# A gather kernel with a sort in front: sort operands made one step ahead, a new dealing of projection blocks, transfers in program order, finer pieces in a compaction, and the last blocks stored singly

## The chip, the core and the metric

The kernel runs on one core of one Trainium2 chip. The metric is the device time of one execution in microseconds (us): the median of three runs before the change is 1930.67 us (1929.54 to 1931.28). The core has five engines that run in parallel, each with its own queue of instructions in a fixed order: PE (TensorE, matrix products), DVE (VectorE), ACT (ScalarE), POOL (GpSimd) and SP (SyncE, which here only starts transfers). An instruction waits at the head of its queue until the semaphores that it needs are set, and everything behind it on that engine waits too.

## The reference, cut to what matters

There are 8192 nodes with 512 features, and 131072 edges sorted by `dst`. The part that the change touches is the graph layer:

```python
def _L0_gnn_ref(x, weight, row, col, vals):
    h = jnp.einsum('nf,ef->ne', x, weight)
    msgs = vals[:, None] * h[col]
    out = jax.ops.segment_sum(msgs, row, num_segments=N_NODES)
    return out
...
x = x + _L0_gnn_ref(_layernorm(x, axis=-1), L0_gnn_weight, src, dst, edge_weight)
x = x + _L0_ffn_ref(_layernorm(x, axis=-1)[None], L0_ffn_W, L0_ffn_b)[0]
```

Every node is normalised and projected to h. Then each edge gathers row `dst` of h, scales it by the edge's weight and adds it to node `src`. Edges come sorted by `dst`, and the sum runs over `src`: the kernel must first sort the edges by `src`. The second layer, a small network on each node's features, follows.

## The kernel before

Nodes lie in 64 blocks of 128. The edges of a block are handled as tiles of 128 slots: 17 tiles for each block, 1088 in all, dealt in two parts (`TILES`: 6 tiles of each block in part 0, 11 in part 1). A tile is one gather of 128 rows of h by POOL (`rows_for`, L519), one selection matrix `hot` made by DVE (`hots_for`, L530), and one 128x512 product on PE (L804). The edges are sorted in two parts as well: part 0 of the sort must be complete before the first gather, part 1 before the first tile of part 1.

The program has three stages in time.

*Head.* `project` computes h for 64 blocks. For a pair of blocks, `load` (L451, SP) fetches 512 KB of x, `scale` takes the statistics on DVE (L459, L460, L171, L463) and normalises on ACT (L170, L465). For each block, `turn` transposes on PE (L474) and copies back on ACT (L476); then come the product on PE (L492), a copy out of PSUM on ACT (L494), and for every second block a store of the pair to `h_rows` (L496, SP). `scale` of a pair is called two blocks ahead of its use, `turn` one block ahead. Steps of the generator `order(0)`, the sort's part 0, are put between these blocks.

*First half of the tiles.* `begin` runs part 0's 384 tiles and puts steps of `order(1)` between them, one step at a tile number `due` that each step moves on (by 3 for `STEP`, 4 for `SLOW`).

*Second half.* `evenly` runs part 1's 704 tiles and the second layer between them.

`order(part)` is a number of chunks, 7 in part 0 and 9 in part 1, followed by `squeeze`. A chunk (`chunk`) makes a one-hot `hot` (L251, DVE), sums it over partitions (L259, PE, copied on ACT at L261), runs a cumulative sum on DVE (L264, L266), takes ranks (L271 on PE, L275 and L277 on DVE), then makes `at` for the whole chunk at once (L281, DVE). Four times over (`SUB` of 2 out of `GC` = 8) it makes `blocks` (L288, ACT), two halves of `put` (L295, DVE), and after the next step 64 short products p_c (L308, PE). `blocks` and `put` have two buffers each. `squeeze` compacts what the chunks placed: a scan (L323), and for each of ten bits a shift (L375), a mask operation (L381), a copy on ACT (L379) and two predicated copies (L387), all but the copy on DVE. `parts` says into how many pieces DVE's instructions are cut: 1 for all of part 0; for part 1, 8 in the chunks and 4 in `squeeze`. At its end `squeeze` transposes the results (L421).

PE, DVE and ACT run in the order in which the program is written. SP and POOL are not in that list (`manual_schedule`, L535): a scheduler decides their order. In the head, a credit says how many steps of the sort go behind each block: 6 for a block from the third on, a step of a chunk costs 3 (two steps for each block), a step of `squeeze` costs 6 (one for each block). The gathers' tiles, x's pairs and h's blocks share one pool of six buffers (`gp`); `gw`, the projection's weights, has one of the two buffers of `xp1`, in which `begin` keeps its x.

Of the kernel before, what the change touches and what calls it, by code (L numbers as in the profile page):

```python
# [17 lines left out]
PE, DVE, ACT = mybir.EngineType.PE, mybir.EngineType.DVE, mybir.EngineType.Activation  # L18

# [14 lines left out]
def tile_gnn_ffn(  # L34
# [51 lines left out]
    STEP, SLOW = 3, 4  # L86
# [158 lines left out]
    def chunk(ck, ps_c, q, col, parts):  # L245
# [9 lines left out]
        yield STEP  # L255
# [6 lines left out]
        yield STEP  # L262
# [4 lines left out]
        yield STEP  # L267
# [5 lines left out]
        yield STEP  # L273
# [5 lines left out]
        for cs in cut(CG, parts):  # L279
            n = cs.stop - cs.start  # L280
            nc.vector.tensor_tensor(  # L281
                at[:, cs].rearrange("p n h s -> p n (h s)"),
                lots.rearrange("p (o h) s -> p o (h s)", o=1).to_broadcast([P, n, CAP]),
                slot[:, cs].to_broadcast([P, n, CAP]), OP.is_equal)
        p_c = None
        for c0 in range(0, GC, SUB):
            blocks = ck.tile([P, SUB, GQ, NB], F32, name="blocks", bufs=2)
            nc.scalar.copy(blocks, hot[:, c0 : c0 + SUB].rearrange("p c b g -> p c g b"))  # L288
            put = ck.tile([P, SUB * GQ, 2, 2, HALF], F32, name="put", bufs=2)
            for i, val in enumerate((val_a, val_w)):  # L290
                for cs in cut(SUB, min(parts, SUB)):
                    n = (cs.stop - cs.start) * GQ
                    v = val[:, q, c0 + cs.start : c0 + cs.stop, :].rearrange(
                        "p c (g a b) -> p (c g) a b", a=1, b=1)
                    nc.vector.tensor_tensor(  # L295
                        put[:, cs.start * GQ : cs.stop * GQ, :, i, :],
                        at[:, (c0 + cs.start) * GQ : (c0 + cs.stop) * GQ],
                        v.to_broadcast([P, n, 2, HALF]), OP.mult)
            yield STEP
            if p_c is None:  # L300
                p_c = ps_c.tile([P, GQ, 2, HALF], F32, name="p_c")
                nc.tensor.matmul(p_c.rearrange("p g w s -> p (g w s)"), nil[:, :P], nil,
                                 start=True, stop=False)
            for k in range(SUB * GQ):
                c, g = divmod(k, GQ)
                last = c0 + SUB == GC and k == SUB * GQ - 1
                for h in range(2):
                    nc.tensor.matmul(p_c[h * NB : (h + 1) * NB, g], blocks[:, c, g, :], put[:, k, h],  # L308
                                     start=False, stop=last)
        for i, cells in enumerate((cells_a, cells_w)):  # L310
# [3 lines left out]
    def squeeze(part, sq, ps_q, parts):  # L314
# [19 lines left out]
        yield SLOW  # L334
# [8 lines left out]
        yield SLOW  # L343
# [22 lines left out]
        yield SLOW  # L366
        wt = cells_w
        for bit in range(LOW, LOW + BITS):
# [14 lines left out]
            yield SLOW  # L383
# [5 lines left out]
            yield SLOW  # L389
# [25 lines left out]
        yield SLOW  # L415
        for f, to in ((dst_f, at_dst[part]), (row_f, at_row[part]), (w_c, at_w[part])):
# [12 lines left out]
            yield SLOW  # L429

    def order(part):
# [7 lines left out]
        with tc.tile_pool(name="sq", bufs=1) as sq, \  # L439
                tc.tile_pool(name="ps_q", bufs=2, space=PSUM) as ps_q:  # L440
            yield from squeeze(part, sq, ps_q, (fine + 1) // 2)


    def project():
# [37 lines left out]
        for b in range(NB):  # L482
# [12 lines left out]
            if b % 2:  # L495
                nc.sync.dma_start(rows_of(h_rows, b - 1, 2), t[:, 2:4])  # L496
                del pairs[b - 1], parts[b - 1]
# [37 lines left out]
    man_ctx.enter_context(tc.manual_schedule(engines={PE, DVE, ACT}))  # L535
    first, second, heads = order(0), order(1), project()
    LEAD, MORE = 2, 2 * STEP
    credit, early = 0, 0
    for b, _ in enumerate(heads):
        credit += MORE if b >= LEAD else 0  # L540
        while credit > 0 and first:
            n = next(first, None)
            if n is None:
                first = None
            else:
                credit -= n if n == STEP else MORE
        if first is None and early < AHEAD:
            hots_for(early)
            early += 1
    assert first is None  # L550
# [257 lines left out]
    def begin():  # L808
# [3 lines left out]
        def load(b0):  # L812
            t = xp1.tile([P, G, D], F32, name="xg")
            nc.sync.dma_start(t, rows_of(x, b0, G))
            return t

# [7 lines left out]
        xs, last = {0: load(0)}, None  # L824
        for b, k, p_g in blocks_of(0):
            t = b * TILES[0] + k
            if k == AFTER and b % G == 0 and b + G < NB:
                xs[b // G + 1] = load(b + G)
            if k == AFTER and last:
                add(*last)  # L830
            if k == TILES[0] - 1:
                last = (b, p_g)
            if t == due:
                due += next(second, NB * FT)
# [249 lines left out]
```

## Time and profile before

| | |
|---|---|
| median of three runs | 1930.67 us |
| the profiled execution | 1927.51 us, 1.8 us of it around its span |
| its span | 1925.7 us |
| busy shares | PE 88%, POOL 58%, DVE 52%, ACT 20% |
| L519 gathers, POOL | 1088 of 1013 ns, 743.4 us idle before them, 691.6 us of it "issue" |
| L804 tile products, PE | 2176 records (two for each tile), 1071.9 us busy |
| L492 projection, PE | 512 records (eight for each block), 238.3 us busy |
| L308 p_c, PE | 4096 records, 140.4 us busy, 28.9 us idle before them |
| L288 blocks, ACT | 64 of 2075 ns |
| store of a pair of h, 512 KB | 3.0 us to landing (median) |
| load of x in `begin`, 1024 KB | 9.1 us to landing (median) |

A line of a timeline reads: start, duration, engine, line, operation, what it writes and reads, shapes, how many were merged, and in brackets the idle time before it and what ended it. A line of the waits reads: who waited for whom, total us, times, longest. A line of the windows reads: the stretch, its length, then for each engine busy us and instructions, TensorE's granted clock, the DMA engines' share and GB/s. The first L251 of the sort starts at 28.99 us, the last product of the head ends at 418.7 us, the first gather starts at 427.14 us, the last gather at 1871.7 us. The span before the first gather is the head; in 427 to 780 us the chunks of part 1 run, from 780 to 905 us its `squeeze`.

### The profile page before, as it was taken

Reading aid. Unit: us, or ns where it says so; the run is one execution under the profiler, and the core shown is the slowest. Engines: PE = TensorE matmul, PEld = TensorE weight load, DVE = VectorE, ACT = ScalarE, POOL = GpSimd, SP = SyncE. Lnnn points to the kernel's source line nnn. Section 1 sums busy time; section 2 is a strip of 40 time slices with the busy share of each in tenths; the row PEclk is TensorE's granted clock in tenths of the full one; section 3 lists DMA queues with packets and bytes.
Section 4 is the critical chain, followed back from the end, with each engine's and each line's share of the span. In section 5 each row is a group of like instructions: output and inputs, shape, how many; then the busy total and the mean of one; then the engine's idle time right before and its main releaser. Section 6 shows DMA issues by size and latency. Waiting matters only on the chain.

```text
span 1925.7 us, 24263 instructions
## 1 busy us (share of the span) xinstructions
PE 1695.5 (88%) x9288; PEld 819.9 (43%) x9288; DVE 1008.2 (52%) x2710; ACT 389.3 (20%) x520; POOL 1124.8 (58%) x1138
## 2 busy tenths in 40 slices
PE   5888889969999999878878789898988989899996
PEld 2554554434455455323333334343434434343454
DVE  5556558635886886985323344435344443434432
ACT  3444545532222222111000011020100101010211
POOL 4000000017777777887777777777777777777760
PEclk9899999989999999978999999899999999999996
DMA  5112223337777777668889777878787787878770
GB/s 177 61 51 67 67 66 115 126 116 219 255 245 237 254 223 223 212 195 257 273 253 321 211 209 223 286 210 295 209 287 220 238 263 209 275 210 274 239 236 25
DMA packets 140908, 391.38 MB, mean 203 GB/s; under 512 B 20336, under 2 KB 21360, under 8 KB 140784
## 3 DMA queue, kind: packets, MB, share of 16 engines
q0 software_dynamic: 87952, 286.45, 49.3%
q1 hardware_dynamic: 52304, 102.25, 15.2%
q8 instruction: 76, 1.25, 0.3%
q10 hardware_dynamic: 528, 1.05, 0.2%
q14 instruction: 48, 0.39, 0.1%
HBM read 339.33 MB, written 50.33 MB: 202 GB/s over the span
## 4 chain that ended last, share of the span: by engine, by line
PE 40%; POOL 19%; DMA 17%; issue 12%; DVE 9%; ACT 3%; POOLq 0%; DVEq 0%; ACTq 0%; SPq 0%
POOL g L519 19%; DMA g<-h_rows,at_dst 16%; PE p_g L804 16%; PE p_g L492 10%; PE p_c L308 6%; DVE cum L264 2%; DVE cum L266 2%; PE p_g L474 2%; ACT blocks L288 1%; DVE at L281 1%; PE p_base L259 1%; PE p_a L603 1%; PE p_a L601 1%; DVE hot L530 1%; PE p_rank L271 1%
## 5 line engine op out<-in xcount | busy, mean ns | idle before, releaser
L519 POOL DMA_INDIRECT g<-h_rows,at_dst x1088 | 1101.9, 1013 | 743.4 <-issue 691.6
L804 PE MATMUL p_g<-g,hot 128*128 128x512 f32 x2176 | 1071.9, 630 | 1.3 <-DVE xg L819 1.3
L804 PEld LDWEIGHTS p_g<-g,hot 128*128 128x128 f32 x2176 | 400.5, 197 | 385.1 <-issue 371.7
L530 DVE TENSOR_SCALAR hot<-lanes,at_row,at_w 128x128 f32<-128x128 f32 x1088 | 302.8, 361 | 158.7 <-PE p_g L804 152.8
L492 PE MATMUL p_g<-xg,g 128*128 128x512 f32 x512 | 238.3, 610 | 1.1 <-ACT g L476 1.0
L308 PE MATMUL p_c<-put,blocks 128*64 128x40 f32 x4096 | 140.4, 236 | 28.9 <-ACT blocks L288 21.8
L800 PE MATMUL p_j<-g,hot 128*1 128x4 bf16 x272 | 45.7, 168 | 135.9 <-DMA g<-h_rows,at_dst 95.6
L308 PEld LDWEIGHTS p_c<-put,blocks 128*64 128x64 f32 x4096 | 132.9, 145 | 70.6 <-ACT blocks L288 33.8
L288 ACT CAST blocks<-hot 128x1024 f32<-128x1024 bf16 x64 | 130.4, 2075 | 136.9 <-issue 111.8
L800 PEld LDWEIGHTS <-hot 128*1 128x1 bf16 x272 | 21.6, 79 | 317.2 <-issue 284.6
L492 PEld LDWEIGHTS p_g<-xg,g 128*128 128x128 f32 x512 | 95.7, 197 | 100.3 <-issue 96.5
L575 DVE TENSOR_SCALAR hb<-p_b,b_b 128x128 f32<-128x128 f32 (+1 forms) x54 | 18.2, 336 | 218.5 <-PE p_b L595 195.9
L264 DVE TENSOR_TENSOR cum<-cum,hot 128x512 bf16<-128x512 bf16 x112 | 47.7, 426 | 118.5 <-ACT cum L261 115.2
L170 ACT ACTIVATE rstd_f<-mv_f,eps 128x8 f32<-128x8 f32 (+1 forms) x9 | 2.7, 300 | 462.6 <-DVE mv_f L788 462.6
L860 DVE TENSOR_TENSOR xu<-xu,p_g 128x512 f32<-128x512 f32 x64 | 43.7, 683 | 84.5 <-PE p_g L804 84.4
L295 DVE TENSOR_TENSOR put<-at,val_a 128x320 f32<-128x320 bf16 (+1 forms) x100 | 54.9, 578 | 59.1 <-PE p_c L308 58.9
L819 DVE TENSOR_TENSOR xg<-xg,p_g 128x512 f32<-128x512 f32 x64 | 43.8, 684 | 70.9 <-PE p_g L804 70.9
L578 ACT ACTIVATE ha<-p_a,b_a 128x512 f32<-128x512 f32 (+1 forms) x54 | 34.5, 640 | 217.0 <-PE p_a L603 206.3
L474 PE MATMUL p_g<-ident,g 128*128 128x128 f32 x256 | 43.2, 296 | 21.5 <-ACT g L465 21.5
L494 ACT COPY g<-p_g 128x512 f32<-128x512 f32 x64 | 37.5, 586 | 119.1 <-PE p_g L492 119.1
L603 PEld LDWEIGHTS p_a<-hb,w_z 128*128 128x128 f32 x360 | 51.8, 207 | 17.9 <-issue 16.7
L295 DVE TENSOR_TENSOR put<-at,val_w 128x320 f32<-128x320 bf16 (+1 forms) x100 | 55.2, 580 | 0.0
(179 smaller groups left out, 1098.1 us busy)
## 6 DMA issues: line engine op xcount, KB each, us to landing
g<-h_rows,at_dst POOLq DMA_INDIRECT x1088, 4.1
g<-in_x_dram SPq DMA_DIRECT2D x32, 512.0 KB, 4.3
xg<-in_x_dram SPq DMA_DIRECT2D x16, 1024.0 KB, 9.1
h_rows<-g SPq DMA_DIRECT2D x32, 512.0 KB, 3.0
x_rows<-xg SPq DMA_DIRECT2D x32, 512.0 KB, 4.4
xu<-x_rows SPq DMA_DIRECT2D x16, 1024.0 KB, 15.6
out_dram<-xu SPq DMA_DIRECT2D x7, 2048.0 KB, 11.0
xg<-in_gnn_wT_dram ACTq DMA_DIRECT2D x1, 1024.0 KB, 9.0
```

Of the source, the lines that this page charges most:

```text
L264: nc.vector.tensor_tensor(cum[:, c], cum[:, c - 1], hot[:, c - 1], OP.add)
L288: nc.scalar.copy(blocks, hot[:, c0 : c0 + SUB].rearrange("p c b g -> p c g b"))
L295: nc.vector.tensor_tensor(put[:, cs.start * GQ : cs.stop * GQ, :, i, :], at[:, (c0 + cs.start) * GQ : (c0 + cs.stop) * GQ], v.to_broadcast ...
L308: nc.tensor.matmul(p_c[h * NB : (h + 1) * NB, g], blocks[:, c, g, :], put[:, k, h], start=False, stop=last)
L474: nc.tensor.transpose(p_t[:, k * P : (k + 1) * P], t[:, 2 + b % 2, k * P : (k + 1) * P], ident)
L492: nc.tensor.matmul(p_h, t[:, b % 2, k * P : (k + 1) * P], gw[:, k, :], start=(k == 0), stop=(k == KD - 1))
L519: nc.gpsimd.indirect_dma_start(out=g[:, k, :], out_offset=None, in_=h_rows, in_offset=bass.IndirectOffsetOnAxis(ap=at_dst[part][:, i : i + ...
L530: nc.vector.tensor_scalar(hot[:, k, :], lanes, at_row[part][:, i : i + 1], at_w[part][:, i : i + 1], op0=OP.is_equal, op1=OP.mult)
L603: nc.tensor.matmul(p_a[:, g, :], w_z[:, i, g, :], last_hb, start=False, stop=((g + 1) * T % 512 == 0 or g == NG - 1))
L800: nc.tensor.matmul(p_j[:, part, :], hot[:, GS - 1, :].bitcast(BF16)[:, 1:2], g.rearrange("p k d -> p (k d)").bitcast(BF16).rearrange("p (k ...
L804: nc.tensor.matmul(p_g, hot[:, i, :], g[:, i, :], start=(k == 0), stop=(k == TILES[part] - 1))
L819: nc.vector.tensor_add(xg[:, b % G, :], xg[:, b % G, :], p_g)
```

## The change

Five things change, and nothing else.

1. *Operands of p_c.* A new inner function `prepare(c0)` makes the piece of `at` that belongs to `c0`, `blocks` and `put`. Two are prepared before the first p_c, and each p_c run prepares the one two further on. `at` is cut into a quarter of the chunk each time.
2. *Dealing of steps in the head.* Each yield carries a second number, the blocks of h that are to run before the next step. In a chunk: 1 behind `hot`, 0 behind L259, 2 behind the cumulative sum, 0 behind the ranks' products, 2 behind the first two `prepare`, then 0, 1, 0 between p_c runs: six blocks for each chunk. In `squeeze`, half a block for each step. Part 1 still goes by the first number, which is unchanged.
3. *SP in program order.* SP is added to the engines whose order is as written. x's first tile of `begin` is loaded behind block 32 of h; the other loads come behind `add`.
4. *`squeeze` of part 1 in 8 pieces*, not 4. Part 0 stays whole.
5. *Blocks 62 and 63 of h are stored singly*, 256 KB each. (The `del` of two dictionary entries goes too; it issues nothing.)

```diff
-        yield STEP
+        yield STEP, 1
...
         cum = ck.tile([P, GC, NB, GQ], BF16, name="cum")
         nc.scalar.copy(cum[:, 0], p_base)
-        yield STEP
+        yield STEP, 0
...
-        yield STEP
+        yield STEP, 2
         p_rank = ps_c.tile([P, GC, NB // GC, GQ], F32, name="p_rank")
...
-        yield STEP
+        yield STEP, 0
         rank = ck.tile([P, GC, GQ], F32, name="rank")
...
-        for cs in cut(CG, parts):
...
-        p_c = None
-        for c0 in range(0, GC, SUB):
+        ready = {}
+
+        def prepare(c0):
+
+            if c0 >= GC:
+                return
+            n = SUB * GQ
+            n0 = c0 * GQ
+            for cs in cut(n, max(1, parts * SUB // GC)):
+                cs = slice(n0 + cs.start, n0 + cs.stop)
+                m = cs.stop - cs.start
+                nc.vector.tensor_tensor(
+                    at[:, cs].rearrange("p n h s -> p n (h s)"),
+                    lots.rearrange("p (o h) s -> p o (h s)", o=1).to_broadcast([P, m, CAP]),
+                    slot[:, cs].to_broadcast([P, m, CAP]), OP.is_equal)
             blocks = ck.tile([P, SUB, GQ, NB], F32, name="blocks", bufs=2)
             nc.scalar.copy(blocks, hot[:, c0 : c0 + SUB].rearrange("p c b g -> p c g b"))
-            put = ck.tile([P, SUB * GQ, 2, 2, HALF], F32, name="put", bufs=2)
+            put = ck.tile([P, n, 2, 2, HALF], F32, name="put", bufs=2)
...
+            ready[c0] = blocks, put
+
+        prepare(0)
+        prepare(SUB)
+        p_c = ps_c.tile([P, GQ, 2, HALF], F32, name="p_c")
+        yield STEP, 2
+        nc.tensor.matmul(p_c.rearrange("p g w s -> p (g w s)"), nil[:, :P], nil, start=True,
+                         stop=False)
+        for c0 in range(0, GC, SUB):
+            blocks, put = ready.pop(c0)
             for k in range(SUB * GQ):
...
+            prepare(c0 + 2 * SUB)
+            if c0 + SUB < GC:
+                yield STEP, c0 // SUB % 2
...
-        yield SLOW
+        yield SLOW, SHARE
...
-            yield from squeeze(part, sq, ps_q, (fine + 1) // 2)
+            yield from squeeze(part, sq, ps_q, fine)
...
-            if b % 2:
+            if b >= NB - 2:
+                nc.sync.dma_start(rows_of(h_rows, b, 1), t[:, 2 + b % 2 : 3 + b % 2])
+            elif b % 2:
                 nc.sync.dma_start(rows_of(h_rows, b - 1, 2), t[:, 2:4])
-                del pairs[b - 1], parts[b - 1]
...
-    man_ctx.enter_context(tc.manual_schedule(engines={PE, DVE, ACT}))
+    man_ctx.enter_context(tc.manual_schedule(engines={PE, DVE, ACT, SP}))
...
-    LEAD, MORE = 2, 2 * STEP
-    credit, early = 0, 0
+    LEAD = 2
+    due, early = LEAD, 0
     for b, _ in enumerate(heads):
-        credit += MORE if b >= LEAD else 0
-        while credit > 0 and first:
-            n = next(first, None)
-            if n is None:
+        while first and due <= b + 1:
+            step = next(first, None)
+            if step is None:
                 first = None
             else:
-                credit -= n if n == STEP else MORE
+                due += step[1]
...
+        if b == NB // 2:
+            x_0 = load_x(0)
...
-        xs, last = {0: load(0)}, None
+        xs, last = {0: x_0}, None
         for b, k, p_g in blocks_of(0):
             t = b * TILES[0] + k
-            if k == AFTER and b % G == 0 and b + G < NB:
-                xs[b // G + 1] = load(b + G)
             if k == AFTER and last:
                 add(*last)
+            if k == AFTER and b % G == 0 and b + G < NB:
+                xs[b // G + 1] = load_x(b + G)
```

With `SHARE` = 0.5. As built, the changed program's queues differ from the old ones as follows. In the head, PE has a chunk's seven pieces as: L259, two blocks, L271, two blocks, two p_c runs, a block, two p_c runs, and a block before the next L259. On SP, the third pair of x comes before x's first tile of `begin` and no longer behind it, that tile stands between two transfers of the middle of the head, and the last h stores stand in front of the next x load and no longer around it. From there on SP's order is the one of before, and so is POOL's.

## The prediction

> **What bounds the kernel now.** I read the busy time by stage first, to see which engine is full where; then the waits of the stage that the change rewrites; then the timelines at the places where one stage hands over to the next.
>
> ```profile
> core 0: us, PE busy (x) PEld busy (x) DVE busy (x) ACT busy (x) POOL busy (x), PEclk, DMA share, GB/s
> 31.60:276.00 244.40, 206.18 (x2180) 127.43 (x2179) 144.95 (x223) 116.85 (x144) 0.00 (x0) 0.93 0.19 63
> 276.00:418.80 142.80, 138.08 (x474) 67.03 (x472) 95.62 (x197) 72.48 (x129) 0.00 (x0) 0.99 0.34 111
> 427.10:780.00 352.90, 328.08 (x2976) 170.40 (x2977) 259.18 (x704) 84.16 (x64) 268.58 (x247) 0.98 0.76 234
> 780.00:905.00 125.00, 95.87 (x190) 37.87 (x190) 102.82 (x260) 13.13 (x10) 103.07 (x73) 0.85 0.69 215
> 905.00:1872.00 967.00, 875.36 (x3218) 385.60 (x3217) 379.05 (x1254) 82.39 (x136) 729.58 (x770) 0.97 0.80 248
> ```
>
> From 905 us to the last gather POOL issues 770 gathers in 967 us, 1.256 us each, and the waits of that stage say that it waits for nobody; 0.3 us each is its own issue:
>
> ```profile
> POOL g L519 <- issue: 204.1, 670, 0.3
> ```
>
> So the last third of the argument is simple: POOL's chain, once saturated (from about 765 us), carries any earlier or later moment to the end one for one. What counts is when the first gather starts, and what POOL loses before 905 us. Before the first gather PE is the longest engine, but with 38.2 us idle in the stage of the chunks (244.4 - 206.2), at a granted clock of 0.93. Who makes it wait there (the two largest):
>
> ```profile
> PE p_c L308 <- ACT blocks L288: 19.3, 13, 2.5
> PE p_rank L271 <- DVE cum L266: 14.1, 6, 2.4
> ```
>
> **Head, chunks.** Before, one chunk took 34.8 us (L302 starts at 81.73 and again at 116.55 us) with four blocks of h in it. PE's work for a block is 3.44 (L492) + 0.44 (L474) = 3.88 us; L259 and L271 1.74 us each (68.00 to 69.74, 76.12 to 77.86); a p_c run 1.99 us (66.01 to 68.00), four of them; L302 0.25. Chunk with four blocks: 15.5 + 3.5 + 8.0 + 0.25 = 27.2, so 7.6 us lost. After, six blocks: 23.3 + 3.5 + 8.0 + 0.25 = 35.0 us, and the waits go:
> - L271 gets two blocks (7.8 us) instead of one to cover L261, L264 and L266 (0.6 + 3.2 + 2.3 = 6.1 us). Gone.
> - The first p_c runs get two blocks to cover rank, slot, at, put (0.7 + 0.2 + 2 x (0.75 + 1.5) = 5.4 us) and two L288 (4.0 us). Gone. The last two get one block and a p_c run, 5.9 us, against 4.5 us of DVE; ACT's second L288 waits for the second p_c run and ends 2.0 us after it. Gone.
> - New: ACT's two L288 (4.0 us) stand ahead of the copies L476 that PE needs for the next block but one; and the statistics of the next pair stand behind the cumulative sum. Following the queues I get 0.15 + 0.85 + 1.3 = 2.3 us of PE's waiting for each chunk.
> Period 37.4 us (35.0 if nothing waits, 39.5 if these waits double). The first L259 stays where it is, at 31.57 us: before it stand the same three blocks. The last p_c run ends 33.5 us into its chunk: 31.6 + 6 x 37.4 + 33.5 = 289.5 us, against 279.9 before; but 44 blocks of h are behind it instead of 30.
>
> **Head, squeeze.** Here the change turns against itself. Half a block for a step puts one bit of the squeeze on each block:
>
> ```profile
> 299.66 0.74 DVE L375 TENSOR_SCALAR go<-word 128x1120 int32<-128x1120 int32 x1
> 300.44 1.33 DVE L381 SCALAR_TENSOR_TENSOR word<-go,word 128x1120 int32<-128x1120 int32 x1
> 301.68 0.69 DVE L459 BATCH_NORM_STATS2 st_h<-g 128x6 f32<-128x512 f32 x1
> ...
> 304.88 1.44 DVE L387 COPY_PREDICATED word<-go,word 128x1118 int32<-128x1118 int32 x1
> 306.22 1.40 DVE L387 COPY_PREDICATED w<-go,w 128x1118 f32<-128x1118 int32 x1
> 307.65 0.74 DVE L375 TENSOR_SCALAR go<-word 128x1120 int32<-128x1120 int32 x1
> ```
>
> A bit is 2.0 us (299.66 to 301.68) + 2.8 us (304.88 to 307.65) = 4.8 us; the statistics of a pair 2.05 us and 0.36 us for ACT's root. Before, two blocks took 8.0 us and held one bit: 4.8 + 2.05, so DVE fitted. Now two blocks hold two bits: 9.6 + 2.4 = 12.0 us against PE's 7.8. DVE is the bound, since PE's next transposes need the statistics queued behind the bits. On DVE from 290.2 us: three opening steps with one pair's statistics 11.6 us, to 301.8; bits 0 to 9 (seven of 4.8, then 4.5, 4.1, 2.7 by the same rows) with five pairs' statistics, 44.9 + 12 = 56.9 us. The statistics of blocks 56 and 57 are the last that PE waits for, two bits' steps earlier: 356 us; ACT's normalising and transposes, then nine blocks to the end (nine products, eight transposes, 34.5 us), 2 us for L421, and 1 us for the transposes' waits seen before: 394.0 us against 418.7. Gain 24.7 us, of about 38 that the idle time offered.
>
> TensorE's clock drops after gaps: at 380.96 us PE had waited 2.26 us and then 0.52, and the eight products behind it took 5.40 instead of 3.44 us. In the squeeze the gaps are some 4 us for each pair, hidden as DVE is the bound; only the last counts, 2 us at most, within the range.
>
> [...]
>
> **Head, last store and SP.**
>
> ```profile
> 418.76 0.37 SPq L814 DMA_DIRECT2D xg<-in_x_dram  x1
> 419.38 0.36 SPq L496 DMA_DIRECT2D h_rows<-g  x1
> ```
>
> ```profile
> 419.38 6.73 DMA h_rows<-g
> ```
>
> The last store is issued behind a 1 MB load that was waiting for `gw`'s buffer, and lands in 6.73 us where the median is 3.0. After, it stands ahead of that load and is half as long: I take 2.4 us (between 2, and 3.0 for the whole pair alone), a gain of 4.3. The load now meets the first gathers; the first four take 3.85 us to issue and 3.9 to land, so it is nearly past (it took 6.0 us there): 0 to 1 us, I take 0. x's first tile moves from SP's first transfers to block 32: at the start DVE waits only for src (until 5.40 us) and then never for x, so nothing is gained; at block 32 it can make the next pair 3 us late, with 8 us of cover: 0 (at worst 3). SP then waits in order, but for stores and loads in the same order as before: 0.
>
> First gather: 427.1 - 24.7 - 4.3 = 398.1 us. **29.0 us gained.**
>
> **Part 1's chunks.** Steps keep their places. PE loses 7.2 us in nine waits for put (0.8 us each), since all of `at` (3.39 us) stands before the first put; with a quarter of it (0.84) these go. POOL waited 11.8 us for PE's buffers there, some 8 beyond its 0.3 a piece: it can take the gain, from the first such wait at about 650 us. I take 6 us (0 to 8). The wait of L271 stays.
>
> **Part 1's squeeze in eighths.** DVE's predicated copies hold up POOL's gathers:
>
> ```profile
> 827.64 2.01 DVE L387 COPY_PREDICATED word<-go,word 128x388 int32<-128x388 int32 x4
> 827.82 4.51 POOL L519 DMA_INDIRECT g<-h_rows,at_dst  x1 [0.30 <-issue]
> 829.54 2.01 DVE L387 COPY_PREDICATED w<-go,w 128x388 f32<-128x388 int32 x4
> ```
>
> A gather that should take 0.95 us ends 0.9 us after the run's last piece: it got into none of the seven gaps. Seven of ten bits cost 2.8 to 3.7 us so, 23 us in all; two passed (pieces of 384 and 304: 1.15 and 1.23 us at most), and the last lost 1 us (176). Pieces of 196 cost about 0.30 us (four of 176: 1.11 us together, four of 391: 2.03), so a run of 16 takes 4.7 instead of 4.0 us. Bounds: all seven stalls gone, 23 us less; all ten stalled and longer, 10 us more. Nearest row: 176, which still waited to its run's end. I take 1 us more. DVE's own extra, some 1 us a bit, is covered: POOL needs 13.8 us for the eight tiles of a stalled bit (8 x 1.25, 3.3, and 0.5 beside L375), DVE 9.4.
>
> The Trainium skill (SBUF — State Buffer, "SBUF: two separate sides") says that whichever of VectorE's and GpSimd's instructions starts first holds the port pair they share for the whole instruction. Read piece by piece, a gather would wait for one piece only, already at four pieces; the 4.51 us row disagrees. If it held for smaller pieces, the time would be 1873 us.
>
> **Sum.** -24.7 - 4.3 - 6 + 1 = -34.0. The profiled execution, 1927.5, gives 1893.5; the median of the runs lies 3.2 above it: 1930.7 - 34.0 = 1896.7, I say 1896 us. Own range of this case: 1885 to 1908 (half of what the chunk's bounds of 35.0 and 39.5 give over seven, -8 and +7, and 3 to 5 us for part 1).
>
> **Rivals.**
> - *POOL gets in between the smaller pieces* (for: the runs that passed; against: seven that didn't). 24 us less: 1873 us.
> - *DVE-bound squeeze is longer*: pairs of 14.5 us rather than 12, as ACT's copies L379 stand ahead of its root (DVE waited 1.2 us for it, at 296.6 us, before), and the clock lost at 10 us. For: those rows; against: PE's 4 us slack a pair. 6 x 2.5 + 3: about 1914 us.
> - *The dealing doesn't remove the waits*, which move to ACT, the chunk at 42 us: seven times 4.6 more, gain gone: 1928 us.
> - *Slower: eighths starve POOL through the whole bit.* Place: 780 to 905 us. If with twice as many instructions no gather passes during L381's pieces either, each bit blocks 1 + 2.4 + 4.7 = 8 us: 80 us over ten bits instead of 27, so 1896 + 53 = 1949 us. It decides from 3.5 us more a bit. Against: beside L381's four pieces gathers passed at 0.99 and 1.12 us.
>
> **How the numbers follow.** Forecast 0.68, POOL freed 0.12, longer squeeze 0.12, no removal 0.03, starved 0.05. A measurement here can tell 0.2% from no change, 4 us. Faster 0.92, same 0.03, slower 0.05. Range for 8 in 10: from 1876, near the freed case, to 1910, near the longer squeeze.
>
> **What would show it.** The first gather near 398 us (390 to 408); L302 every 37 us with PE's waits for L288 and L266 nearly gone in the chunks; PE waiting for L465 in the squeeze; the last h store landing in under 3 us; no wait for put from there to 780 us minus the shift; POOL still with gathers of over 4 us in L387's runs, or without. The forecast is wrong if the first gather stays above 415 us, or if POOL loses more than 60 us in `squeeze`.

## The result, and the profile after

The changed kernel takes 1902.64 us (median of six runs, 1899.08 to 1906.19), beside 1930.11 us for the kernel before on the same chip: ratio 0.986, 95% interval 0.9843 to 0.9877. The forecast was 1896 us. The profiled executions are 1903.79 and 1927.51 us, their spans 1901.9 and 1925.7 us: 23.8 us less. The medians lie 27.5 us apart: the execution of before that was profiled lies 2.6 us below its median, that of the change 1.2 us above.

To place these 23.8 us I cut both traces at the same gathers of POOL: the first, the 220th after it (the last chunks of part 1's sort), the 320th after it (the end of its squeeze), and the last.

| stretch, us | before | after | difference | forecast |
|---|---|---|---|---|
| start to the first gather | 427.1 | 399.5 | -27.7 | -29.0 |
| 220 gathers on, beside part 1's chunks | 312.6 | 303.4 | -9.2 | -6 |
| the next 100, beside part 1's squeeze | 167.0 | 176.5 | +9.5 | +1 |
| from there to the last gather | 965.0 | 966.4 | +1.4 | 0 |
| last gather to the end | 54.0 | 56.2 | +2.2 | 0 |
| sum | 1925.7 | 1901.9 | -23.8 | -34.0 |

The busy time by stage, after. The first row is the chunks of the head, the second the head's squeeze, then part 1's chunks, its squeeze, and the rest.

```profile
core 0: us, PE busy (x) PEld busy (x) DVE busy (x) ACT busy (x) POOL busy (x), PEclk, DMA share, GB/s
31.60:286.00 254.40, 245.36 (x2405) 142.07 (x2403) 159.42 (x280) 141.07 (x190) 0.00 (x0) 1.00 0.28 93
286.00:395.70 109.70, 88.36 (x251) 41.01 (x249) 85.51 (x161) 47.47 (x82) 0.00 (x0) 0.94 0.24 82
399.40:720.00 320.60, 305.06 (x2805) 159.41 (x2806) 241.15 (x668) 80.99 (x63) 243.80 (x232) 0.98 0.79 246
720.00:880.00 160.00, 119.56 (x372) 49.69 (x371) 129.48 (x428) 18.07 (x18) 126.89 (x89) 0.86 0.66 199
880.00:1846.00 966.00, 869.99 (x3201) 382.13 (x3199) 378.43 (x1251) 81.33 (x132) 728.85 (x768) 0.97 0.79 247
```

In the head's chunks PE's idle time fell from 38.2 to 9.0 us (254.4 - 245.4), and the granted clock rose from 0.93 to 1.00. In the head's squeeze it is the other way: PE had 4.7 us of idle time there before (142.8 - 138.1), now 21.3. The waits of PE up to the last product of h say for whom:

```profile
PE p_g L490 <- ACT g L481: 15.4, 6, 3.4
PE p_g L508 <- ACT g L492: 12.2, 20, 0.8
```

The waits for `blocks` and `cum`, 19.3 and 14.1 us in the chunks before, are gone. The second line is the new wait in the chunks, two short ones (0.52 and 0.78 us) in each chunk, and the 0.52 us behind each longer gap of the squeeze. The first is the squeeze of the head: PE waits for ACT's normalising, which waits for DVE. PE's timeline there (start, duration, engine, line, what; the idle time before it in brackets):

```profile
306.14 0.66 PE L490 MATMUL p_g<-ident,g 128*128 128x128 f32 x4 [2.47 <-ACT g L481]
307.31 5.40 PE L508 MATMUL p_g<-xg,g 128*128 128x512 f32 x8 [0.52 <-ACT g L492]
312.55 0.60 PE L490 MATMUL p_g<-ident,g 128*128 128x128 f32 x4
312.99 3.60 PE L508 MATMUL p_g<-xg,g 128*128 128x512 f32 x8
319.03 0.66 PE L490 MATMUL p_g<-ident,g 128*128 128x128 f32 x4 [2.45 <-ACT g L481]
320.20 3.70 PE L508 MATMUL p_g<-xg,g 128*128 128x512 f32 x8 [0.52 <-ACT g L492]
```

This pair of blocks takes 12.9 us (306.14 to 319.03), and the product behind its gap runs for 5.40 us, the next one for 3.60. Not every gap does that: behind the next, of 2.45 us, the product runs for 3.70 us, and that pair takes 12.1 us (319.03 to 331.13). Of the six gaps for L481 four are followed by a slow product (5.19 to 5.40 us, behind 2.68, 2.47, 3.36 and 2.39 us) and two are not (3.70 us, behind 2.45 and 2.10 us). The five pairs between them take 12.9, 12.9, 12.1, 12.6 and 12.5 us. DVE and ACT in the pair from 306.14:

```profile
305.15 0.74 DVE L391 TENSOR_SCALAR go<-word 128x1120 int32<-128x1120 int32 x1
...
310.24 0.74 DVE L391 TENSOR_SCALAR go<-word 128x1120 int32<-128x1120 int32 x1
...
314.39 1.43 DVE L403 COPY_PREDICATED w<-go,w 128x1116 f32<-128x1116 int32 x1 [0.59 <-ACT w L395]
315.71 0.68 DVE L475 BATCH_NORM_STATS2 st_h<-g 128x6 f32<-128x512 f32 x1
...
318.04 0.74 DVE L391 TENSOR_SCALAR go<-word 128x1120 int32<-128x1120 int32 x1
```

```profile
312.75 0.59 ACT L510 COPY g<-p_g 128x512 f32<-128x512 f32 x1 [3.49 <-PE p_g L508]
313.23 1.13 ACT L395 COPY w<-w 128x1120 f32<-128x1120 f32 x1
317.44 0.29 ACT L171 ACTIVATE rstd_h<-mv_h,eps 128x2 f32<-128x2 f32 x1 [3.08 <-DVE mv_h L476]
```

One bit takes 5.1 us (305.15 to 310.24), the next 5.5 with a wait of 0.59 us for ACT's copy, and the statistics 2.3 us (315.71 to 318.04). DVE is nearly full, as forecast, but each piece is a little longer than I had put it, and ACT's copy for the second bit stands behind the copy of the slow product's result. Of the four pairs with two whole bits (from 306.14, 319.03, 331.13 and 343.76), DVE waits for that copy in the three with a slow product (0.6, 0.4 and 1.3 us) and not in the one from 319.03.

The end of the head, on SP's queue and on POOL:

```profile
396.31 0.33 SPq L512 DMA_DIRECT2D h_rows<-g  x1
396.68 0.43 SPq L557 DMA_DIRECT2D xg<-in_x_dram  x1
399.47 1.01 POOL L536 DMA_INDIRECT g<-h_rows,at_dst  x1 [375.33 <-issue]
```

The last store now goes ahead of the 1 MB load. The first gather starts 3.8 us after h's last product ends (395.65); before it was 8.4 us.

Part 1's squeeze, one bit, DVE and POOL:

```profile
754.53 2.28 DVE L403 COPY_PREDICATED word<-go,word 128x195 int32<-128x195 int32 x8
...
755.52 4.27 POOL L536 DMA_INDIRECT g<-h_rows,at_dst  x1 [0.30 <-issue]
...
756.71 2.28 DVE L403 COPY_PREDICATED w<-go,cells_w 128x195 f32<-128x195 int32 x8
...
758.89 1.11 DVE L547 TENSOR_SCALAR hot<-lanes,at_row,at_w 128x128 f32<-128x128 f32 x4
```

The gather starts among sixteen predicated copies and ends at 759.79, 0.90 us after the operation behind the last of them starts (758.89). Smaller pieces have not let it in. Eight copies take 2.28 us where four took 2.01, and both runs of a bit 4.4 us (754.53 to 758.89) where they took 3.8 (827.64 to 831.43), so the stop is longer. Not every gather in such a run is held: three that start in one (the 277th, 278th and 303rd after the first) take 1.02 to 1.10 us. Below, "held" is the sum, over the gathers 200 to 340, of what each takes beyond 0.95 us, counted for those of more than 1.2 us: 38.1 us before, 43.3 after.

Longer gathers are not all of the 9.5 us. For the 100 gathers beside the squeeze, 6.0 us lie in their own durations (138.4 us in sum, 132.4 before) and 3.5 us in POOL's idle time, nearly all of it in one place at the squeeze's opening. There the scan (L339), also cut into eighths, takes 5.2 us (731.27 to 736.50) where quarters took 4.2 (768.10 to 772.32). PE waits for its result for 3.0 us instead of 2.0, and its next six product records run for 4.54 us instead of 2.84. POOL waits for a buffer that these products free, first in the changed kernel, then before:

```profile
742.14 1.23 POOL L536 DMA_INDIRECT g<-h_rows,at_dst  x1 [4.33 <-PE p_g L828]
776.26 1.95 POOL L519 DMA_INDIRECT g<-h_rows,at_dst  x1 [0.97 <-PE p_g L804]
```

### The profile page after: what moved, and what is told of

It reads as the page before. It is cut to its first block, busy times and chain, and to the rows that moved or that the text cites. A ratio compares the mean times of both kernels' runs of the same rounds, so it can differ in the third digit from the quotient of the medians.

```text
span 1901.9 us, 24398 instructions
## 1 busy us (share of the span) xinstructions
PE 1682.3 (88%) x9288; PEld 807.2 (42%) x9288; DVE 1021.4 (54%) x2863; ACT 388.6 (20%) x520; POOL 1123.2 (59%) x1138
## 4 chain that ended last, share of the span: by engine, by line
PE 36%; POOL 21%; DMA 18%; issue 12%; DVE 7%; ACT 5%; POOLq 0%; DVEq 0%; ACTq 0%
POOL g L536 21%; DMA g<-h_rows,at_dst 18%; PE p_g L828 16%; PE p_g L508 7%; PE p_c L321 6%; DVE cum L265 2%; DVE cum L267 2%; PE p_base L260 1%; ACT blocks L296 1%; ACT g L481 1%; PE p_a L627 1%; DVE st_h L475 1%; PE p_rank L272 1%; PE p_a L625 1%; PE p_g L490 1%
## 5 line engine op out<-in xcount | busy, mean ns | idle before, releaser
L824 PE MATMUL p_j<-g,hot 128*1 128x4 bf16 x272 | 45.7, 168 | 143.3 <-DMA g<-h_rows,at_dst 91.6
L321 PEld LDWEIGHTS p_c<-put,blocks 128*64 128x64 f32 x4096 | 123.5, 138 | 34.7 <-issue 27.1
L321 PE MATMUL p_c<-put,blocks 128*64 128x40 f32 x4096 | 129.4, 230 | 0.0
L291 DVE TENSOR_TENSOR at<-lots,slot 128x320 bf16<-128x320 bf16 (+1 forms) x100 | 55.2, 580 | 0.6
```

Of the source, the lines that this page charges most:

```text
L291: nc.vector.tensor_tensor(at[:, cs].rearrange("p n h s -> p n (h s)"), lots.rearrange("p (o h) s -> p o (h s)", o=1).to_broadcast([P, m, C ...
L824: nc.tensor.matmul(p_j[:, part, :], hot[:, GS - 1, :].bitcast(BF16)[:, 1:2], g.rearrange("p k d -> p (k d)").bitcast(BF16).rearrange("p (k ...
```

## The experiments

The first four kernels ran together on a chip on which everything behind the head was slower (the kernel before took 2227.6 us there, at a granted clock of 0.89 instead of 0.95 over its runs; why is open), so of these I read the ratio, the head, and stretches of the four beside each other; the gathers' own 0.95 us were the same there.

**The squeeze in quarters again, and whole.** Two kernels, each with one line of the change turned back or driven on:

```diff
-            yield from squeeze(part, sq, ps_q, fine)
+            yield from squeeze(part, sq, ps_q, (fine + 1) // 2)
```

> The changed kernel with part 1's squeeze in four pieces again, all else as changed. Theory A (a gather caught by the predicated copies waits until the last piece of the whole back-to-back run, and eight pieces make the run longer and catch more gathers): gathers in the squeeze wait 4.3 to 4.6 us again where they waited 4.3 to 5.2, the 80 gathers from the 220th to the 300th take some 139.6 us as before the change instead of 146.9, and the time is 1893 us (9 to 10 us less). Rival B (the loss after the 220th gather only gives back what part 1's chunks gained, because POOL was about to be the limit there anyway): the time stays at 1902 us whatever the pieces.

```diff
-            yield from squeeze(part, sq, ps_q, fine)
+            yield from squeeze(part, sq, ps_q, 1)
```

> The changed kernel with part 1's squeeze in whole instructions (1568 elements, about 1.9 us each by the rows of 391 and 1120 elements), so two predicated copies for a bit and no boundary inside either. Theory A (a run holds a gather to its end): the run is 3.7 us instead of 4.0 with four pieces and 4.7 with eight, waits of 3.5 to 4.5 us, the time 1889 to 1892 us. Rival C (a gather waits for the piece that runs, and enters at the next boundary): waits up to 1.9 us for each long instruction, those of the mask operation too, and the time is either far lower, about 1880 us, if the two copies let a gather in between, or above that of four pieces if every one of four long instructions a bit catches a gather.

Quarters: 2182.12 us, ratio 0.9787 (0.9748 to 0.9827), first gather at 399.7 us, held 36.1 us with nine gathers over 2.2 us. Whole: 2180.69 us, 0.9796 (0.9749 to 0.9843), first gather 400.6, held 45.8 us with thirteen. The times of the two can't be told apart, nor from the eighths of the next kernel (2180.52). What can be read is the 100 gathers beside the squeeze: 181.2 us in quarters (417.9 to 599.1 after the first gather), 185.5 whole, against 188.7 and 189.1 with eighths in the next two kernels. With whole instructions neither theory holds alone: gathers that start beside the two copies last to 0.8 us after the end of the second (up to 4.36 us), as theory A says, and four of 2.22 us stand beside one whole `scalar_tensor_tensor` of 1.8 us (in three of them the mask's), as rival C says of the mask. Quarters are the shortest of the three, by about 7 us against eighths, and have the least held (43.9 us with the eighths of the next kernel). That agrees with the +9.5 us above, but on this chip it doesn't prove it.

**A larger share of a block for a step of the head's squeeze.**

```diff
-    STEP, SLOW, SHARE = 3, 4, 0.5
+    STEP, SLOW, SHARE = 3, 4, 0.65
```

> The changed kernel with 0.65 instead of 0.5 blocks of h for each step of part 0's squeeze, so that its 27 steps lie beside 17.5 blocks instead of 13.5. Theory D (DVE is the bound in the head's squeeze: 12 us of its work for two blocks of 7.8 us of PE; spread further, both fit): PE's waits for the normalisation shrink from 15 us to under 5, TensorE's slow products with them, the last product of h ends at 374 to 380 us instead of 395.7, the first gather starts at about 380, the time is 1880 to 1886 us. Rival E (PE waits for ACT's own chain of copies, not for DVE's load): the waits stay for each pair, now over more pairs, the first gather stays near 399 us, the time 1902 us.

First gather at 389.8 us, 9.7 us before the changed kernel's; 2180.52 us, ratio 0.9784 (0.9747 to 0.9821). PE's waits:

```profile
PE p_g L508 <- ACT g L492: 11.1, 18, 0.8
PE p_g L490 <- ACT g L481: 9.8, 4, 2.7
```

The waits for ACT's L481 fell from 15.4 to 9.8 us, with two gaps fewer. That is theory D's direction with half its size or less: it gave waits under 5 us and a first gather at about 380 us. The head's squeeze is bound by DVE at half a block for a step, and the first gather can come earlier by starting the same steps further apart.

**The operands ahead, with the old dealing.** The credit loop of before drives the changed chunk.

```diff
-    due, early = LEAD, 0
+    MORE = 2 * STEP
+    credit, early = 0, 0
...
-        while first and due <= b + 1:
+        credit += MORE if b >= LEAD else 0
+        while credit > 0 and first:
...
-                due += step[1]
+                credit -= step[0] if step[0] == STEP else MORE
```

> The changed kernel with the head's old dealing (two steps of a chunk, one of the squeeze for each block), operands still made one step ahead. Theory F (the operands made ahead remove most of the chunk's waits by themselves, and the new dealing gives in the squeeze what it gains in the chunks): a chunk of four blocks takes 31 to 32 us instead of 34.8, with the wait of the ranks' product for the cumulative sum (2.35 us each) still there and that for blocks gone; the squeeze runs at 4.0 us a block again; the last product of h ends at 385 to 392 us, the time is 1892 to 1899 us. Rival G (the new dealing is what removes the waits): the chunk stays above 33 us, the last product ends at 400 us or later, the time is 1907 us or more.

First gather at 420.8 us, last product of h at 416.9; 2205.82 us, ratio 0.9891 (0.9853 to 0.9928). The waits of the head are back:

```profile
PE p_c L321 <- ACT blocks L296: 17.2, 7, 2.5
PE p_rank L272 <- DVE cum L267: 16.4, 7, 2.4
```

So the last product comes 1.8 us earlier than before (418.7), and 21.3 us later than in the changed kernel: in the head it is the dealing that takes the waits away, since operands that are ready in time for a step are worth little while the same two steps stand in the same block as the work they wait for.

**Eighths in the kernel before.** The other way round: before, with nothing but the eighths.

```diff
-            yield from squeeze(part, sq, ps_q, (fine + 1) // 2)
+            yield from squeeze(part, sq, ps_q, fine)
```

> The kernel before with one thing of the change: part 1's squeeze in eighths. Theory H (a gather waits to the end of a whole back-to-back run of predicated copies, and a run of eight takes 2.28 us where a run of four takes 2.01, so that finer pieces only lengthen each stop): some 9 us slower than before, ratio 1.005; the gathers of over 1.2 us among the 200th to 340th lose 42 to 48 us in sum (38 before), and none of the long ones becomes shorter. Theory I (the 9.5 us that the changed kernel lost there come from where its steps fall among the tiles, as its first gather and its chunks moved, not from the size of the pieces): within 3 us of before, ratio 0.9985 to 1.0015, sum 36 to 40 us.

1936.87 us beside 1926.77 of before: ratio 1.0055 (1.0035 to 1.0074), some 10 us slower. The 100 gathers beside the squeeze take 175.8 us (167.0 in before, 176.5 in the changed kernel), held 45.7 us. The eighths alone cost nearly what the changed kernel lost there, so theory I, that the loss came from where the steps fall, falls. Theory H explains the larger part: of the 8.7 us, 7.0 lie in the gathers' durations, and 1.7 in POOL's wait at the scan (2.63 us, 0.97 before). In this kernel the six product records behind the scan ran for 2.84 us; the slow ones of the changed kernel account for the rest of its wait.

**The same pieces, alternating.**

```diff
-            for cs in cut(n, parts):
-                nc.vector.scalar_tensor_tensor(stay[:, cs], ...)
-            yield SLOW, SHARE
-            for to, of in ((stay, word), (w2, wt)):
-                for cs in cut(m, parts):
-                    ...
-                    nc.vector.copy_predicated(to[:, cs], go[:, ds], of[:, ds])
+            keeps, moves = cut(n, parts), cut(m, parts)
+            if parts > 1:
+                half = parts // 2
+                for i in range(half):
+                    keep(keeps[i])
+                    move(stay, word, moves[i])
+                yield SLOW, SHARE
+                for i in range(half, parts):
+                    keep(keeps[i])
+                    move(stay, word, moves[i])
+                    for j in (2 * (i - half), 2 * (i - half) + 1):
+                        move(w2, wt, moves[j])
```

`keep` is the masked piece (`scalar_tensor_tensor`), `move` the predicated copy of one piece.

> The changed kernel, and in part 1's squeeze the pieces of the masking (scalar_tensor_tensor) and of the predicated copies alternate: one masked piece, then one, later three, copied pieces of 0.28 us, where before 16 copies stood in a row; the same instructions and steps, the head unchanged (first gather 399 to 400 us). Theory H (the whole run holds the gather, and a masked piece between two copies lets it in): no gather of over 2.2 us in the squeeze (11 in the changed kernel), the sum over 1.2 us falls from 43 to under 12 us, and the time by 25 to 32 us: ratio 0.970 to 0.973 if the changed kernel's is 0.986. Theory I2 (every copy holds the gather, however they stand): the sum stays at 40 to 46 us and the ratio at 0.984 to 0.988. Theory J (with copies spread over the whole bit a gather is held for the bit): the sum rises to 70 us or more, ratio over 0.998.

1872.64 us, ratio 0.9718 (0.9696 to 0.9739). The 100 gathers take 143.2 us instead of 176.5, and held is 10.4 us, with one gather over 2.2 us. In its timeline:

```profile
769.76 0.95 POOL L553 DMA_INDIRECT g<-h_rows,at_dst  x1 [0.30 <-issue]
769.88 0.38 DVE L402 COPY_PREDICATED word<-go,word 128x196 int32<-128x196 int32 x1
770.16 0.64 DVE L402 COPY_PREDICATED w<-go,w 128x196 f32<-128x196 int32 x2
770.71 0.35 DVE L397 SCALAR_TENSOR_TENSOR word<-go,word 128x196 int32<-128x196 int32 x1
771.02 0.95 POOL L553 DMA_INDIRECT g<-h_rows,at_dst  x1 [0.30 <-DMA g<-h_rows,at_dst]
```

DVE is as busy as in the stalled bit, yet each gather shown takes its 0.95 us, and none beside the copies more than 2.0 us. The 33.3 us are all in the gathers' durations (105.0 us in sum, 138.4 in the changed kernel); POOL's wait at the scan is still 4.32 us. With the same instructions and the same sizes, only their order changed: it is the run of copies without another operation that held POOL, not the copies' number or size. The order also brings a short pause: the copy behind a masked piece needs its result and starts 0.03 us after its end (769.85 to 769.88), where copies in a row overlap. Whether this pause or the other operation lets the gather in is not shown. The one gather left (2.51 us) stands beside a chunk's one-hot (L252), before the squeeze.

**Quarters and the larger share together.** Both edits shown above.

> The changed kernel with the squeeze in quarters again and 0.65 of a block for a step of the head's squeeze where it has 0.5. If both gains are real and add: first gather at 389.8 us (9.7 earlier, as with 0.65 alone), and the gathers 220 to 320 some 9 us shorter than 176.5: 1903 - 9.7 - 9.0 = 1884 us where before is 1930, ratio 0.976. Rival (the quarters' 9 us were a matter of where steps fall): the head's gain alone, ratio 0.981.

1883.77 us, ratio 0.9775 (0.9754 to 0.9796); first gather 391.8 us (389.8 expected); 166.8 us beside the squeeze, as in before (167.0). Both gains are real and add.

**Operands not ahead, with the new dealing.**

```diff
         prepare(0)
-        prepare(SUB)
...
-            prepare(c0 + 2 * SUB)
+            prepare(c0 + SUB)
```

> The changed kernel's dealing of blocks, but blocks and put made right before their products' step and not one step ahead. Theory K (the dealing alone removes the head's waits, the operands ahead matter only in part 1): first gather 397 to 402 us, PE's wait for put in part 1's chunks back at 9 times some 0.8 us, gathers 0 to 220 at 309 to 313 us (303.4 in the changed kernel). Theory L (both are needed in the head too: two of the four runs have no block or one behind their operands' step): PE waits again for blocks, some 4 to 6 us for each chunk, first gather at 425 to 440 us.

One run: 1920.14 us. First gather at 404.3 us, between the two theories: 4.9 us after the changed kernel's (0.9 of them before the sort's first product), with PE's waits for `blocks` at 8.1 us in fourteen places of at most 0.6 us. Part 1 is what neither theory foresaw: 220 gathers take 324.3 us, 20.9 more than in the changed kernel and 11.7 more than in before, and PE has no wait for `put`. The loss is on POOL. This kernel's timeline:

```profile
543.20 0.88 DVE L291 TENSOR_TENSOR at<-lots,slot 128x320 bf16<-128x320 bf16 x2
543.85 2.67 POOL L535 DMA_INDIRECT g<-h_rows,at_dst  x1 [0.30 <-issue]
544.01 0.88 DVE L303 TENSOR_TENSOR put<-at,val_a 128x320 f32<-128x320 bf16 x2
544.81 0.89 DVE L303 TENSOR_TENSOR put<-at,val_w 128x320 f32<-128x320 bf16 x2
545.62 1.11 DVE L546 TENSOR_SCALAR hot<-lanes,at_row,at_w 128x128 f32<-128x128 f32 x4
```

and the changed kernel's, for the same kind of run:

```profile
568.29 0.93 DVE L303 TENSOR_TENSOR put<-at,val_w 128x320 f32<-128x320 bf16 x2
568.29 0.94 POOL L536 DMA_INDIRECT g<-h_rows,at_dst  x1 [0.30 <-issue]
569.14 0.92 DVE L291 TENSOR_TENSOR at<-lots,slot 128x320 bf16<-128x320 bf16 x2
569.53 0.95 POOL L536 DMA_INDIRECT g<-h_rows,at_dst  x1 [0.30 <-issue]
569.98 0.88 DVE L303 TENSOR_TENSOR put<-at,val_a 128x320 f32<-128x320 bf16 x2
```

In the first, the gather ends at 546.52, 0.90 us after the operation behind the run starts (545.62): held, as in the squeeze, by operations that are not predicated copies. In the second the same pieces let both gathers through at 0.94 and 0.95 us, and DVE's pairs are up to 0.05 us longer where one got in. Of the first 220 gathers 22 take more than 1.5 us here: 14 beside such runs (2.48 to 3.13 us) and eight beside the chunk's one-hot (L252, up to 3.41 us). In the changed kernel there are only eight, all beside the one-hot (2.51 us). So a run can hold a gather and need not. What decides it stays open. The two gathers that passed start within 0.01 us of a piece's start, the one that was held 0.24 us into a piece; but in this kernel others that start 0.17 to 0.30 us into one pass at 1.01 to 1.14 us.

**SP's order, and the pair of last blocks.** Two kernels, each with one of the two parts of the store undone.

```diff
-    man_ctx.enter_context(tc.manual_schedule(engines={PE, DVE, ACT, SP}))
+    man_ctx.enter_context(tc.manual_schedule(engines={PE, DVE, ACT}))
```

> The changed kernel with SP's order left to the scheduler again: the same on the other engines, but the load of x's second 1 MB tile stands ahead of the last single store of h again, and the first 1 MB tile at SP's start. Theory M (that order was the cost of the last store): first gather 402.5 to 405 us, 3 to 5 us after the changed kernel's 399.5 to 401. Rival N (the half size of the last store was): first gather within 1 us of it.

```diff
-            if b >= NB - 2:
-                nc.sync.dma_start(rows_of(h_rows, b, 1), t[:, 2 + b % 2 : 3 + b % 2])
-            elif b % 2:
+            if b % 2:
```

> The changed kernel with the last two blocks of h stored as one pair, in SP's written order. Theory M: first gather some 0.6 us later (3.0 us to landing for a pair against my 2.4 for one block), 400 to 401.5 us. Rival N: 3 us or more later, 402.5 us or after.

With SP's order left to the scheduler, one run gives 1908.03 us and a first gather at 403.1 us. SP's queue has the load ahead of the last store again:

```profile
393.15 0.33 SPq L512 DMA_DIRECT2D h_rows<-g  x1
395.96 0.37 SPq L557 DMA_DIRECT2D xg<-in_x_dram  x1
396.58 0.33 SPq L512 DMA_DIRECT2D h_rows<-g  x1
```

From h's last product (395.93) to the first gather it is 7.2 us, 3.3 more than in the changed kernel. With a pair stored at the end (one run, 1902.49 us, first gather 401.9) it is 4.9 us from the last product at 397.02: 1.1 more. In the ten kernels with both parts this step is 3.78 to 3.85 us, so both differences are clear. That kernel's first gather is 2.5 us later than the changed kernel's, outside what theory M gave, but 1.4 us of it stand before the last product and have nothing to do with the store. 3.3 and 1.1 us make up 4.4 of the 4.6 us by which this step became shorter: theory M holds, with the order as the larger part.

**The best parts together.** Alternating pieces with 0.65, and with 0.72, the last that fits.

```diff
-    STEP, SLOW, SHARE = 3, 4, 0.5
+    STEP, SLOW, SHARE = 3, 4, 0.65
```

> Alternating pieces in part 1's squeeze and 0.65 of a block for a step of the head's squeeze, together. If both gains add: first gather at 390 us (9.7 earlier), no long gathers in the squeeze, ratio 0.9718 - 9.7/1927 = 0.967, some 1863 us where before is 1927. Rival (the earlier start is lost again in the chunks or the squeeze of part 1): ratio 0.970 to 0.973 as without it.

```diff
-    STEP, SLOW, SHARE = 3, 4, 0.5
+    STEP, SLOW, SHARE = 3, 4, 0.72
```

> As the kernel with alternating pieces and 0.65, but 0.72 of a block for a step of the head's squeeze: its 27 steps then end 63.4 blocks in, the last that fits. If the head's loss is PE waiting behind three steps in two blocks (9.8 us left at 0.65, in 4 places): fewer such places, first gather 385 to 388 us, 2 to 5 us less than with 0.65. Rival (the sort now ends too late for the first gather's row numbers): first gather 392 us or later, while the last product of h ends at 386 us or before.

With 0.65: 1860.77 us beside 1928.37 of before, ratio 0.9656 (0.964 to 0.9672), first gather 391.2 (390 expected): the two gains add. With 0.72: 1859.66 us, ratio 0.965 (0.9633 to 0.9667), first gather 387.6, as expected, though PE's waits for the normalising became more places and not fewer (seven instead of five, 9.3 us instead of 10.9). The 3.6 us that the first gather gains are mostly given back in the next hundred gathers (137.1 us for them against 134.8), and the two can't be told apart. Both are some 40 us faster than the changed kernel, by its ratio of 0.986 (0.986 - 0.965 = 0.021, times 1928 is 40.5 us).

## Why the forecast was right, step by step

- *What bounds the kernel.* Right. What the first gather gained and what the squeeze lost both came through to the end, with 3.6 us (1.4 and 2.2) added after the squeeze that no step had. The 2.2 us behind the last gather are of this execution: the eight kernels below that ran after the first four have 53.5 to 54.3 us there, and before has 54.0.
- *Head, chunks.* Forecast 37.4 us for a chunk and 289.5 us for the last p_c run; measured 36.9 us (52.73 to 274.0 for six) and 285.95. The new waits were 1.3 us a chunk, not 2.3. With the gaps gone the granted clock is 1.00 in this stage (0.93 before), which I had not counted. That the dealing does most of it is shown by the two kernels that have one part without the other: h's last product ends at 416.9 us with the operands ahead alone, at 400.5 with the dealing alone, and at 395.65 with both (418.7 before).
- *Head, squeeze.* DVE is the bound, as forecast, but a pair takes 12.1 to 12.9 us, not 12.0: bits of 5.1 to 5.5 us instead of 4.8 in the pair shown, with waits for ACT's copy that stands behind the slow product. From the last p_c run to h's last product it is 109.7 us against 104.5 in my sum. The chunk's gain of 3.6 and this loss of 5.2 us give 395.65 against 394.0: the head came out right because two errors cancelled. The sum let only the last gap cost clock. Four products ran slow, 1.5 to 1.7 us each against the 3.70 us of the full-speed ones behind a gap, and of the pairs with two whole bits the one whose product ran at full speed was the one without a wait for ACT's copy, and came nearest to the sum (12.1 us). So the slow products seem not to have been wholly hidden; how much of the 5.2 us they cost is not separated.
- *Last store.* Forecast -4.3 us, measured -4.6.
- *Part 1's chunks.* Forecast -6 us, measured -9.2, 1.2 outside my bounds of 0 to -8. A chunk took 36.4 us before (gathers held by L251 at 468.64, 505.05, 541.46) and takes 35.6 after (440.67, 476.25, 511.81), and nine times 0.85 is 7.6 us, about the whole wait for `put` (7.2 us). On POOL the same gain is in the gathers' own durations: 231.7 us in sum for the 220, 240.4 before, at the same idle time (71.7 and 72.2 us). My sum had no shorter gathers here. Which of the two engines set the pace, and so which wait was worth the 9.2 us, is argued and not shown: in the kernel without operands ahead PE has no wait for `put` either, and the stage is 20.9 us longer because of POOL.
- *Part 1's squeeze in eighths.* The term that was mis-sized: +1 us forecast, +9.5 measured, near the upper of my two bounds (+10). I weighed the bounds as if some stalls would go. None of the long ones did: the copies of a bit take 4.4 us where they took 3.8, and the three bits that had cost little before held a gather too, which took 2.4 to 2.9 us. The seven stalled bits in before were the row to go by, and the row said that a gather gets into no gap. That makes 6.0 us. The other 3.5 come from a term that I put at nothing, DVE's own extra, which I had called covered: I had worked it out for the bits alone, and at the scan, where eighths cost 1.0 us more, it was not. So the upper bound was met partly by another cause than its own. The Trainium skill's statement (SBUF — State Buffer, "SBUF: two separate sides") that the port pair is held for one whole instruction (of VectorE's it names those in a two-port mode and those with two SBUF inputs) would have had gathers wait for one piece; in the trace they take up to 5.22 us, over a run of sixteen pieces of 0.37 us.
- *The sum.* -34.0 forecast, -23.8 measured between the profiled executions (-27.5 between the medians, which puts 1902.64 us beside my 1896). Of the 10.2 us between them the squeeze in eighths makes 8.5, the rest behind it 3.6, the head 1.3, and part 1's chunks give 3.2 back: that the total is no further off is partly luck.

The rival of POOL freed by smaller pieces (1873 us) did not come. It had the right prize: with the order changed the same pieces do free POOL, and the 100 gathers beside the squeeze take 143.2 us, 23.8 less than before, where the rival gave 23. That the time of that kernel, 1872.64 us, equals the rival's is chance: it was measured on another chip, beside 1926.77 us for the kernel before. The rival of the longer squeeze in the head had the right sign and a quarter of its size (0.6 us a pair in the mean of five, not 2.5). Its 10 us for the clock are what six gaps at the row of 380.96 us would give (5.40 against 3.70 us, 1.7 us each); measured are four slow products, 6.5 us in sum.

## What to carry to other kernels

When one engine holds another up, look at the length of the run of such pieces, not at the size of one: cutting a run finer made it longer here, and putting other work between the pieces took the stall away. Count what finer pieces cost everywhere that the cut reaches: here the scan that opens the squeeze grew by 1.0 us and POOL waited for it. When waits are moved by dealing work differently, work out the stage that gets less cover with the same care as the one that gets more; a share of 0.5 made DVE the bound, and 0.65 gave back 9.7 us. Cut both traces at the same events, and compare stretch by stretch, before saying which part of a change did what.

## What the hardware showed unexpectedly

- A gather that starts within a run of DVE pieces of one kind can last to 0.90 us after the run, whose pieces were 0.37 to 0.6 us each: in predicated copies (5.22 us at most in the changed kernel), and in runs of `at` and `put` products (3.13 us at most, where they were not made ahead). Others that start in such runs pass at 0.95 to 1.14 us. With masked pieces between the copies no gather beside them took more than 2.0 us.
- Behind gaps of 2.1 to 3.4 us on PE in the head's squeeze, the eight records of a product took 5.19 to 5.40 us in four cases and 3.70 us in two; 2.47 us of gap made a slow one and 2.45 us did not. The chunk stage, with gaps of at most 0.8 us, had a granted clock of 1.00.
- Eight predicated copies of 195 elements take 2.28 us, four of 391 take 2.03, so that each further piece costs 0.06 us.
